# Perceiver layer on one core: queries of the scores dealt by ScalarE, the last 65 keys on all partition quarters, loads held back at the start

## The chip, the cores and the metric

One NeuronCore of a Trainium2 chip runs the whole layer. The metric is the device time of one execution in microseconds, as the median of several runs. All data is fp32.

## The reference, cut to what matters

A batch of 8 samples has 64 query rows each and 1,601 context rows (keys) of width 512. The layer is cross attention to the context with one head, a second attention over the 64 rows with 16 heads, and a feed-forward layer that sends every row to one of eight experts.

```python
# x: (8, 64, 512), ctx: (8, 1601, 512)
q = layernorm(x) @ Wq + bq
k = ctx @ Wk + bk;  v = ctx @ Wv + bv
x = x + softmax(q @ k.T / sqrt(512)) @ v
xn = layernorm(layernorm(x)) * ln_w + ln_b       # second attention, 16 heads of 32
qh, kh = l2norm(xn @ Wq2), l2norm(xn @ Wk2)
m = sigmoid(15 * (qh @ kh.T - 0.29514)) * (qh @ gq)[:, None] * (kh @ gk)[None, :]
x = x + (m @ (layernorm(x) @ Wv2)) @ Wo + bo
h = layernorm(x)                                 # experts
e, w = argmax(h @ gate.T), sigmoid(max(h @ gate.T))
x = x + expert_e(w * h)                          # u * silu(g) @ down
```

## The kernel before, in words

The 512 query rows are four tiles of 128 (p = 0 to 3); a tile holds two samples (b2 = 0, 1). The kernel never forms the keys: it computes q Wk^T once for a tile (`keyed`, p_qk, four products against the slab xWkT) and multiplies it with the raw context. The scores of a tile are summed over 16 blocks of 32 context columns, four blocks to a quarter q (`scores`, L369). The context arrives with keys on partitions, in three groups of 512 keys (a load of 1 MB for each sample, twelve keys of a sample on one partition, four of them per group) and a tail of 65 keys (`load_group`, L205 to L217). VectorE turns 32x32 blocks of it (`turn_group`, L231) into the tiles T: partition quarter a of T holds 32 columns by the keys whose row lies in partition quarter a, 384 of them plus the tail's share. The tail lies in partitions 0 to 64 of an array of 96 rows, so the four quarters have 416, 416, 385 and 384 keys (WIDTH, L226). TensorE then runs eight products at once, four row quarters by two samples, into four banks sc.

For that, the queries must stand four times under one another: R has 128 partitions (four quarters of the same 32 columns) by 16 blocks by 128 rows. GpSimd writes each 32 columns of q Wk^T four times side by side (`spread`, L341), TensorE turns 16 such squares (`fill_queries`, L358, rt) and ScalarE copies them to R in four copies (L361). R exists once.

`softmax` (L376) takes the four maxima on VectorE, a bias, and four exponentials on ScalarE into L, with a fifth of one column for key 65. `chances` turns L back (pp, L413), ScalarE copies it (pt, L415), and `attend` multiplies it with the context as it came (ac, L425), group by group. `divided` scales (acs), and the value projection xWv follows one tile later (`at_turn`, `at_out`, p_po).

Arrays live in pools: twelve slabs of 1 MB for weights and context groups, five block arrays (tag blk) for T, L and the blank rows, 22 rows of 256 KB. A load waits until its array is free. TensorE's order is the order in which the program is written; ScalarE's is so only from `keyed(0)` to the transposes of x; the other engines are ordered by a scheduler when the kernel is built. All large loads go through SP's queue, in order, and a load there waits until the eighth before it has landed. Small constants go through GpSimd's queue.

At the start the kernel normalizes x, projects tile 0's queries, forms q Wk^T of tile 0, then projects the other three tiles (`project_q`). VectorE meanwhile turns the first five T arrays of tile 0 as the loads arrive in the order tail, 0, 1, 2; xWv and tile 1's loads follow at once. After the scores of tile 0 come the q Wk^T of tiles 1, 2 and 3. From tile 1 on, the steps of the second attention and of the gate of earlier tiles are set between those of the cross attention: the gate's part (`gate_parts`, shares, L700; `gate`, pl) starts in tile 2.

## Time and profile before

| | us |
|---|---|
| median of 3 runs | 295.79 |
| lowest and highest | 295.11, 296.79 |
| profiled execution, its own time | 295.09 |
| its span | 293.4 |
| TensorE busy | 279.1 |
| VectorE busy | 159.6 |
| ScalarE busy | 93.2 |
| GpSimd busy | 63.9 |

The profile is of one execution. Durations and start times are counted from the start of its span; the execution's own time is 1.69 us longer than the span. A line of the timeline has the start, the duration, the engine (PE is TensorE, PEld its weight load, DVE VectorE, ACT ScalarE, POOL GpSimd, SP the engine of the load queue), the line of the kernel, and what is written from what. A group line has the busy time and the mean of one instruction after the first bar, and the idle time of the engine before them, with what ended it, after the second. A matmul of fp32 appears as two records.

### The profile page before, as it was taken

To read this page: it belongs to the slowest core of one execution; us is meant where nothing else is said; L and a number is where in the kernel's file an instruction comes from. 1 tells how busy PE (TensorE), PEld (TensorE's weight loads), DVE (VectorE), ACT (ScalarE), POOL (GpSimd) and SP (SyncE) were. 2 spreads that over 40 slices of the span, in tenths; PEclk is the share of its full clock that TensorE was granted. 3 is DMA by queue.
4 is the path that set the end of the run, shared out by engine and by line. 5 is a ranking of instruction groups with operands and counts; after the bars stand their busy time and mean duration, and the time that the engine had idled before them with its cause. 6 is when DMAs were issued, how large, how long until landed. Compare 5 with 4: busy or idle time off the path is not lost. (4 is left out here: it accounts for less than half of the span.)

```text
span 293.4 us, 6477 instructions
## 1 busy us (share of the span) xinstructions
PE 279.1 (95%) x2661; PEld 138.3 (47%) x2661; DVE 159.6 (54%) x414; ACT 93.2 (32%) x203; POOL 63.9 (22%) x110
## 2 busy tenths in 40 slices
PE   5689999999999999999999999999999999999991
PEld 5555664633554244655534465534454455343320
DVE  2554487336853477956667794453372466374140
ACT  3221403620037131326714143652425434130110
POOL 4055400600081002500220310022050032413301
PEclk9999999999999999999999999999999999999999
DMA  6999980189974993000199401959991200523401
GB/s 185 348 414 396 344 330 1 32 347 416 386 275 163 359 417 122 4 3 0 29 395 369 142 2 26 370 188 329 376 376 61 74 0 2 158 92 117 175 3 43
DMA packets 20288, 57.71 MB, mean 197 GB/s; under 512 B 2274, under 2 KB 10514, under 8 KB 16544
## 3 DMA queue, kind: packets, MB, share of 16 engines
q1 hardware_dynamic: 17568, 50.37, 47.5%
q0 software_dynamic: 2400, 6.89, 6.3%
q8 instruction: 23, 0.38, 0.5%
q14 instruction: 9, 0.07, 0.1%
q10 hardware_dynamic: 288, 0.00, 0.1%
HBM read 50.94 MB, written 6.84 MB: 197 GB/s over the span
## 5 line engine op out<-in xcount | busy, mean ns | idle before, releaser
L233 DVE STREAM_TRANSPOSE T<-cx 128x512 f32<-128x512 f32 x96 | 61.9, 681 | 25.1 <-DMA cx<-in_ctx_dram 19.4
L369 PE MATMUL sc<-T,R 32*64 32x416 f32 (+2 forms) x1024 | 49.9, 501 | 0.1
L425 PE MATMUL ac<-cx,pt 128*64 128x512 f32 x192 | 43.8, 599 | 0.0
L369 PEld LDWEIGHTS sc<-T,R 32*64 32x64 f32 x1024 | 26.5, 131 | 17.6 <-issue 6.8
L425 PEld LDWEIGHTS ac<-cx,pt 128*64 128x64 f32 x192 | 12.7, 136 | 22.1 <-issue 21.2
L1010 PE MATMUL gu<-wgu,xeT 128*32 128x512 f32 x192 | 22.9, 597 | 0.0
L501 POOL TENSOR_TENSOR gm_k<-qn_k,c_gk 128x512 f32<-128x512 f32 x4 | 5.1, 1284 | 61.4 <-DVE qn_k L496 61.4
L185 PE MATMUL p_qk<-w_xWkT,qpT 128*128 128x512 f32 x32 | 14.2, 598 | 2.9 <-DMA w_xWkT<-in_xWkT_dram 2.9
L464 POOL TENSOR_TENSOR x<-x,c_bo 128x512 f32<-128x512 f32 x4 | 5.1, 1268 | 53.6 <-DVE xh L463 53.6
L341 POOL COPY q<-qk 128x512 f32<-128x512 f32 x16 | 9.0, 615 | 34.0 <-ACT qk L313 34.0
L284 PE MATMUL qp<-xnT,w_xWq 128*128 128x128 f32 (+1 forms) x64 | 14.4, 384 | 1.3 <-ACT xnT L275 1.3
L185 PE MATMUL p_q<-w_aWq,xhT 128*128 128x512 f32 x32 | 14.8, 605 | 0.1
L185 PE MATMUL p_k<-w_aWk,xhT 128*128 128x512 f32 x32 | 14.7, 595 | 0.0
L185 PE MATMUL p_po<-w_xWv,acT 128*128 128x512 f32 x32 | 14.7, 595 | 0.0
L380 DVE TENSOR_REDUCE mx<-sc 128x1 f32<-128x416 f32 (+2 forms) x16 | 8.1, 567 | 11.9 <-PE sc L369 11.9
L185 PE MATMUL p_o<-w_aWo,cT 128*128 128x512 f32 x32 | 14.5, 596 | 0.0
L185 PE MATMUL p_v<-w_aWv,xvT 128*128 128x512 f32 x32 | 14.4, 592 | 0.0
L415 ACT COPY pt<-pp 128x512 f32<-128x512 f32 (+1 forms) x16 | 8.2, 515 | 17.5 <-PE pp L413 15.8
L284 PEld LDWEIGHTS qp<-xnT,w_xWq 128*128 128x128 f32 x64 | 9.7, 191 | 5.7 <-ACT xnT L275 1.8
L1045 PE MATMUL y<-wd,hT 128*32 128x512 f32 x96 | 11.5, 596 | 0.6 <-DVE hT L1037 0.6
L185 PEld LDWEIGHTS p_qk<-w_xWkT,qpT 128*128 128x128 f32 x32 | 5.8, 190 | 10.5 <-issue 7.4
L1020 DVE TENSOR_TENSOR h<-gu,h 128x256 f32<-128x256 f32 x6 | 2.5, 424 | 14.0 <-ACT h L1019 14.0
(198 smaller groups left out, 387.6 us busy)
## 6 DMA issues: line engine op xcount, KB each, us to landing
cx<-in_ctx_dram SPq DMA_DIRECT2D x24, 1024.0 KB, 10.1
wgu<-in_wgT_dram SPq DMA_DIRECT2D x8, 512.0 KB, 9.2
wgu<-in_wuT_dram SPq DMA_DIRECT2D x8, 512.0 KB, 10.0
wd<-in_wdT_dram SPq DMA_DIRECT2D x8, 512.0 KB, 8.4
rd<-blank POOLq DMA_DIRECT2D x6, 258.0 KB, 4.8
in<-rd SPq DMA_DIRECT2D x6, 258.0 KB, 5.0
xd<-blank POOLq DMA_DIRECT2D x6, 256.0 KB, 4.8
in<-xd SPq DMA_DIRECT2D x6, 256.0 KB, 7.2
```

The lines of the kernel that those rows point to most:

```text
L185: nc.tensor.matmul(ps, lhsT=srcT[:, dc, :], rhs=w[:, dc, :], start=(dc == 0), stop=(dc == DC - 1),)
L233: nc.vector.transpose(T[:, :, 128 * g : 128 * g + 128].rearrange("p b (c k) -> p b c k", k=32), cxs[p, g][b2][:, :, 128 * q : 128 * q + 12 ...
L284: nc.tensor.matmul(ps[ec][:, : n * P], lhsT=wq[:, dc, ec * P : (ec + 1) * P], rhs=xnT[:, dc, cols], start=(dc == 0), stop=(dc == DC - 1),)
L341: nc.gpsimd.tensor_copy(q4, qk[:, 32 * b0 : 32 * b0 + 128].rearrange("p (b d) -> p b d", d=32).unsqueeze(2).to_broadcast([P, 4, 4, 32]),)
L369: nc.tensor.matmul(sc[a][r : r + S, : WIDTH[a]], lhsT=R[32 * a : 32 * a + 32, b, r : r + S], rhs=Ts[b2][32 * a : 32 * a + 32, j, : WIDTH[a ...
L380: nc.vector.tensor_reduce(mx[:, a : a + 1], sc[a][:, : WIDTH[a]], AX.X, ALU.max)
L415: nc.scalar.copy(pt[:m, :nch, :], tp[:m, :nch, :])
L425: nc.tensor.matmul(ac[r : r + S, :], lhsT=pt[:m, j, r : r + S], rhs=rhs, start=(g == 0 and j == 0), stop=(g == 3),)
L464: nc.gpsimd.tensor_tensor(xs[i], xs[i], bo, ALU.add)
L501: nc.gpsimd.tensor_tensor(heads(gm), heads(qn), gb.unsqueeze(1).to_broadcast([P, H, HD]), ALU.mult)
L1010: nc.tensor.matmul(ps[c, :], lhsT=xTs[k][:, dc, c], rhs=ffw[e][0][:, dc, :], start=(dc == 0), stop=(dc == DC - 1),)
L1045: nc.tensor.matmul(y[c, :], lhsT=hT[:, ic, c], rhs=ffw[e][1][:, ic, :], start=(ic == 0), stop=(ic == IC - 1),)
```

## The change

Seven edits belong together:

- q Wk^T of tiles 1 to 3 is turned plainly, four transposes for a tile (`turn_queries`), and ScalarE deals it to R: for each partition quarter a, four copies of 32 partitions by 512 (`deal_queries`). Tile 0 keeps the old way.
- q Wk^T of tile 3 is formed in tile 1 instead of tile 0, and ScalarE's order is written by hand from the softmax's end to the end of the attend stage in tiles 0 to 2.
- In tile 0, VectorE's order is written by hand: groups 0, 3 and 1 of tile 1 are turned into four T arrays after the softmax, group 2 around `divided`.
- At the start, the transposes of x for tiles 1 to 3 stand between the two halves of tile 0's q Wk^T.
- The tail is loaded in pieces of 17, 16, 16 and 16 keys to the four partition quarters, so the score widths are 401, 400, 400, 400; the softmax treats it as a 13th column of 128 with zeros, and four small exponentials fill it.
- The tail's loads come behind groups 0 and 1 (four large loads) in tile 0.
- Two slabs are held by a one-column copy on GpSimd that reads the end of qpT, in front of the constants' loads; xWv is loaded after tile 1's context.

```diff
-        [one.tile([96, D], F32, tag=f"tail{k}{b2}", name=f"tail{k}{b2}") for b2 in range(2)]
+        [one.tile([P, D], F32, tag=f"tail{k}{b2}", name=f"tail{k}{b2}") for b2 in range(2)]
-            nc.gpsimd.memset(tails[k][b2][64:96, :], 0.0)
+            nc.gpsimd.memset(tails[k][b2], 0.0)
+    REST = (17, 16, 16, 16)
-                nc.sync.dma_start(out=c[: SK - 12 * P, :], in_=src[12 * P :, :])
+                k0 = 12 * P
+                for a, n in enumerate(REST):
+                    nc.sync.dma_start(out=c[32 * a : 32 * a + n, :], in_=src[k0 : k0 + n, :])
+                    k0 += n
-    for g in (3, 0, 1, 2):
+    for g in (0, 1, 3, 2):
         cxs[0, g] = load_group(0, g)
-    wv = load_w("xWv")
-    WIDTH = (416, 416, 385, 384)
+    WIDTH = tuple(384 + n for n in REST)
...
+    def turn_queries(p):
+        return transposed(qks.pop(p), f"rt_{p}")
+    def deal_queries(R, tp, a):
+        for j in range(4):
+            nc.scalar.copy(R[32 * a : 32 * a + 32, j::4, :], tp[32 * j : 32 * j + 32, :, :])
...
+        nc.gpsimd.memset(L[:, 12, :], 0.0)
...
-        nc.scalar.activation(
-            L[:, 12, 64:65], sc[2][:, 384:385], AF.Exp, bias=bias, scale=scale,
-            accum_out=sm[:, 4:5],
-        )
+        for a, n in enumerate(REST):
+            nc.scalar.activation(
+                L[:, 12, 32 * a : 32 * a + n], sc[a][:, 384 : 384 + n],
+                AF.Exp, bias=bias, scale=scale,
+            )
+        nc.vector.tensor_reduce(sm[:, 4:5], L[:, 12, :], AX.X, ALU.add)
...
-        keyed(0)
-        for i in range(1, NT):
-            turn_x(i, later[i - 1])
+        def turn_later():
+            for i in range(1, NT):
+                turn_x(i, later[i - 1])
+        keyed(0, turn_later)
...
+    for k in range(2):
+        tc.keep_in_program_order(
+            nc.gpsimd.tensor_copy(slab(f"held{k}")[:, 0, 0:1], qpT[:, DC - 1, NT * P - 1 :])
+        )
...
     load_pair(1)
+    wv = load_w("xWv")
...
+        if p > 0:
+            do((at_turn, p - 1))
         L, r = softmax(p, sc)
+        if p == 0:
+            turns = tc.manual_schedule(engines={mybir.EngineType.DVE})
+            turns.__enter__()
+            second = {(q, b2): block_tile(1, q, b2) for q in range(2) for b2 in range(2)}
+            for g in (0, 3, 1):
+                turn_second(g)
+        acts = ExitStack()
+        if p < NT - 1:
+            acts.enter_context(tc.manual_schedule(engines={mybir.EngineType.Activation}))
...
         if p == 0:
             for k in range(1, NT):
-                keyed(k)
-                if k == 1:
-                    q4s = spread(1)
+                if k < NT - 1:
+                    keyed(k)
+            turned_qk = turn_queries(1)
+            R = queries(1)
             tables()
...
-        if p + 1 < NT:
+        if p == 0:
+            chance()
+        elif p + 1 < NT:
             R = queries(p + 1)
-            if p == 0:
-                chance()
-                fill_queries(1, R, q4s, 0)
...
+            if p == 1:
+                keyed(NT - 1)
+            do((at_out, p - 1))
+            chance()
+            turned_qk = turn_queries(p + 1)
...
             attend(p, g, pts[g], ac)
+            if p < NT - 1 and g < 3:
+                deal_queries(R, turned_qk, g)
+                if p == 0 and g == 2:
+                    deal_queries(R, turned_qk, 3)
...
+        if p == 0:
+            turn_second(2, (0,))
         tile_of[p]["acs"] = divided(p, ac, r)
+        if p == 0:
+            turn_second(2, (1,))
         if 0 < p < NT - 1:
             do((unit_q, p - 1))
+            deal_queries(R, turned_qk, 3)
+        acts.close()
```

## The prediction

> **What bounds the kernel now.** I read the page's busy table first, then the groups by form, then the timeline around the places that the diff touches.

> ```profile
> PE 279.1 (95%) x2661; PEld 138.3 (47%) x2661; DVE 159.6 (54%) x414; ACT 93.2 (32%) x203; POOL 63.9 (22%) x110
> L369 PE MATMUL sc<-T,R 32*64 32x416 f32 x512 | 49.9, 513 | 0.1
> L358 PE MATMUL rt<-ident,q 128*128 128x128 f32 x64 | 8.0, 272 | 0.0
> L361 ACT COPY R<-rt 128x512 f32<-128x512 f32 x16 | 8.5, 601 | 1.2 <-PE rt L358 1.2
> ```

> PE is busy in 95% of the span, and its groups show almost no idle time before them: TensorE's order of work is the path, and the other engines count only where TensorE would come to wait for them. So I price each edit in TensorE time, and then look for what TensorE meets next. The stage in question is tile 0, from its last score matmul to tile 1's scores (start, duration, engine):

> ```profile
> 45.84 10.57 PE L185 MATMUL p_qk<-w_xWkT,qpT 128*128 128x512 f32 x24
> 45.94 2.02 DVE L380 TENSOR_REDUCE mx<-sc 128x1 f32<-128x416 f32 x4 [3.10 <-PE sc L369]
> ...
> 48.43 0.21 DVE L386 TENSOR_SCALAR bias<-qb,nb 128x1 f32<-128x1 f32 x1
> ...
> 48.72 1.28 ACT L391 ACT_TABLE_LOAD   x1 [15.66 <-DVE bias L386]
> ...
> 52.55 1.09 ACT L313 COPY qk<-p_qk 128x512 f32<-128x512 f32 x2
> ...
> 56.39 0.64 PE L413 MATMUL pp<-ident,L 128*128 128x128 f32 x4
> ...
> 56.86 1.91 PE L358 MATMUL rt<-ident,q 128*128 128x128 f32 x16
> ...
> 59.14 3.65 PE L425 MATMUL ac<-cx,pt 128*64 128x512 f32 x16
> ...
> 71.59 3.80 PE L369 MATMUL sc<-T,R 32*64 32x416 f32 x84
> 71.74 0.75 DVE L432 TENSOR_SCALAR acs<-ac,r 128x512 f32<-128x512 f32 x1 [1.21 <-PE ac L425]
> ```

> The reader is to see that three products p_qk (10.5 us) cover the softmax: its exponentials end at 52.3, pp follows at 56.39 without a wait. At the start the loads set the pace instead. The windows view gives GB/s in its last column:

> ```profile
> 12.00:15.00 3.00, 1.44 (x4) 0.68 (x4) 2.49 (x8) 0.52 (x2) 0.00 (x0) 1.00 1.05 296
> 16.00:20.00 4.00, 3.17 (x17) 2.04 (x16) 2.33 (x8) 2.05 (x4) 2.07 (x4) 1.00 1.02 424
> 32.50:36.50 4.00, 3.95 (x75) 1.87 (x64) 1.31 (x2) 0.30 (x2) 0.17 (x1) 1.00 1.02 284
> ```

> In the first and third of these a pair of 65-row tail loads is in flight, and everything crawls: 296 and 284 GB/s against 424. VectorE's timeline has tile 0's groups arriving 2.5 us apart (turned at 18.55, 21.02, 23.52), then 3.3, 2.8 and 3.2 us apart while GpSimd's constants load; the last is turned at 32.85, and the scores, started at 32.66, stop for it.

> [...] the table load's 1.28 us stands in the trace. [...] a quarter of the scores (64 records) takes 2.95 us start to start here.

> **The change part by part.** Every change of time is against the profiled execution, 295.09 us (span 293.4 and 1.7 around it); the median of the runs, 295.79, lies 0.7 above it.

> 1. *Queries by ScalarE.* Tiles 1 to 3 lose 16 transposes each and gain 4. The 16 take 1.75 us (56.86 to 58.61), four take 0.45: **1.3 us less of TensorE each, 3.9 in all.** ScalarE gets 16 copies of 0.51 us (8.2 us) in place of 4. Their cover is the attend stage, 12.4 us with 1.6 us of other copies in tile 0: three quarters are dealt beside groups 0 to 2, the fourth beside group 2 (tile 0) or the next products (tiles 1, 2). The last copy of tile 0 ends about when its first scores need it: nothing to pay (2.1 us, the last quarter's four copies, if that cover is gone). But in tile 2, four deals (2.1 us) now stand ahead of the square-root table load and the copy of the gate's shares, which today ends 0.04 us before TensorE uses it (145.32, 145.36): **0.7 us of wait.** In tile 1 the same copies have slack, since no gate is computed there. GpSimd's 12 copies of 0.6 us go; they ran beside p_qk and the scores, so nothing.

> 2. *One product p_qk moved from tile 0 to tile 1.* TensorE's sum is the same, but the cover in tile 0 shrinks from 10.5 to 6.95 us. In the changed order four turns of tile 1 (two of 0.66, two of 0.27 us) also stand between the maxima and the bias on VectorE, 1.5 us of them unhidden. From the last score S: bias at S+4.3 (now S+2.8), table load 1.3, four exponentials 2.25, four small ones 0.8 ([...] a lone one takes 0.24 here with its accumulator), copy of the product and hand-over 0.75: S+9.4. TensorE is there at S+6.95: **a new wait of 2.4 us at the transposes of q Wk^T.** Then 0.45 for them, 0.15, pp 0.45 and its copy: attend starts at S+11.2, now at S+13.3, **2.1 us earlier**. Tile 1 pays: between its scores and pp stand 0.5 + 3.47 + 3.47 = 7.45 us instead of 5.3 (which held a 0.45 us wait for the exponentials): **2.15 us later**.

> 3. *Turns of tile 1 ahead.* Group 2 of tile 1 is loaded once tile 0's first attend group frees its buffers, lands 4.9 and 7.4 us later (as the load issued at 56.44 did: turned at 61.37), so the first quarter is ready as the scores start: 0.2 us. Then VectorE has acs (0.75), two turns (1.25) and four blocks of 2.05 us, 10.2 us, before the last quarter can run (2.85): 13.2 us for tile 1's scores instead of 12.2: **1.0 us later.** VectorE becomes the bound there.

> 4. *Narrower scores.* 401 columns for 416: 2.95 becomes 2.85 us a quarter. Eight quarters in tiles 2 and 3: **0.8 us less.** Tiles 0 and 1 wait for VectorE's blocks in their last quarter and keep nothing.

> 5. *Tails, holds and start.* Without the tails in front, groups land earlier by 0.65 us of bytes and 0.85 of lost rate (0 to 1.9 as bounds); the constants move behind qpT, which takes 0.85 us off group 1. So the fourth large load lands at about 24.3. Now a wait is added on SP's queue: the last of eight tail pieces waits for that landing, and group 2's loads stand behind it[...]. Issue at 24.8 to 26, landing 4.9 us later, the second 2.5 after: 32.2 to 33.4, now 32.85. [...] TensorE itself is ready some 1.4 us sooner (the first half of xWkT lands 0.6 earlier; with the transposes between the halves the 0.8 us wait for xnT goes). I take **0.7 us less**, between 1.4 less and 2.5 more. The tails cost SP six more issues a tile of some 0.35 us; its queue has waits of tens of us, so nothing but the stop above. The two held copies on GpSimd wait for qpT (30.6), and behind them the seven constant loads and four additions of xbv move from 20 to 33 us on to about 31 to 43; their first user is tile 0's output sum near 89. Tile 1's loads, xWv and the attention weights come later than now, under tens of us of other work. The output weight and tile 2's first group wait for the moved product; the normalization of tile 1's stage stands behind that group on VectorE, with 1 to 3 us to spare by my count.

> 6. *Softmax details.* A memset of 0.2 us on GpSimd, idle then, and one more reduce beside pp and attend: nothing. Tail transposes and products have as many columns as before: nothing.

> Sum: 1.3 (tile 3's queries) − 0.7 in tile 2; 2.1 − 0.2 in tile 0; −1.0 − 2.15 + 0.45 (queries and their copies after pp) in tile 1; 0.8 for scores; 0.7 at the start: **1.3 us less**. 295.09 − 1.3 = 293.8 in the profile, **294.5** as median. Of 5.4 us taken off TensorE's work, three new waits take most back.

> **The rivals.** *The cover holds.* If maxima, turns and exponentials overlap better, and the blocks of tile 1 arrive in time, 2.4 + 1.0 and half of the 0.7 us of waits vanish: 3.75 us more, 290.8. For it: the exponentials end 4 us before pp today. Against: the product's copy stands behind the exponentials on ScalarE. *The start gets slower.* Group 2 issued behind the tail pieces: [...] the last group lands at 35.4, 2.5 us late. The rest of the sum gives 0.6, so 1.9 us slower: 297.7. It decides from a landing at 35.0. For it: issue waits in order on SP; against: the crawl at 296 GB/s ends. *The edits don't pay in TensorE time*: the array's rate isn't set by the width, and tile 2's first group comes late: 295.8.

> **How the numbers follow.** Forecast 0.46 (own range 292.9 to 296.1), cover holds 0.22, slower start 0.22, no gain 0.10. The bound for a difference that a measurement of this kernel can tell is about 0.5%, 1.5 us: 294.3 and 297.3. Half of the forecast's chance lies below 294.3, the rest within; with the rivals: faster 0.46, same 0.30, slower 0.24. Leaving out one in ten on each side gives 290.6 to 297.8.

> **What would show it.** Right: a wait of some 2 us of the transposes t_rt for ScalarE's copy of qk in tile 0; the scores of tile 1 over 13 us, waiting for VectorE's T; 12 fewer query transposes in each of tiles 1 to 3; no stretch under 300 GB/s at 12 to 15 us, but a dip near 25 to 27. Wrong: the first scores starting after 34, or pp of tile 0 within 9 us of the last score.

## The result and the profile after

| | before | changed |
|---|---|---|
| median, us | 295.27 (20 runs) | 296.41 (20 runs) |
| lowest to highest, us | 294.04 to 297.12 | 294.39 to 298.27 |
| profiled execution, its span, us | 295.09, 293.4 | 296.17, 294.4 |

The changed kernel takes 1.0035 times as long, with an interval of 1.0014 to 1.0055: about 1.0 us slower, where 1.3 us less was forecast. Ratios here are of undisturbed executions alone, so a ratio can differ from that of two medians.

The busy table and the groups of the changed kernel show that the edits did what they say:

```profile
PE 277.9 (94%) x2625; PEld 134.9 (46%) x2625; DVE 160.5 (55%) x418; ACT 116.0 (39%) x247; POOL 58.1 (20%) x104
...
L382 PE MATMUL sc<-T,R 32*64 32x400 f32 (+1 forms) x1024 | 50.7, 516 | 3.2 <-DVE T L237 2.2
...
L374 ACT COPY R<-t_rt 32x512 f32<-32x512 f32 x48 | 27.6, 576 | 0.8
```

TensorE has 36 records fewer (12 transposes for each of three tiles), and ScalarE has 48 deals. But the score group now has idle time ahead of it, 3.2 us in all, 2.2 of them on VectorE's T. TensorE's timeline shows where (start, duration, engine, line, what is written from what, count; in brackets the idle time just before, and what ended it). First the kernel before, then the changed one:

```profile
32.66 3.97 PE L369 MATMUL sc<-T,R 32*64 32x416 f32 x64
36.57 0.33 PE L332 MATMUL t_qb<-ident,qbT 128*128 128x128 f32 x1
```
```profile
29.78 1.08 PE L324 MATMUL qb<-qpT,c_xbk 128*32 128x128 f32 x32
31.05 0.85 PE L382 MATMUL sc<-T,R 32*64 32x401 f32 x2 [0.19 <-DVE T L237]
33.96 4.63 PE L382 MATMUL sc<-T,R 32*64 32x401 f32 x62 [2.05 <-DVE T L237]
38.52 0.33 PE L336 MATMUL t_qb<-ident,qbT 128*128 128x128 f32 x1
...
47.70 7.13 PE L185 MATMUL p_qk<-w_xWkT,qpT 128*128 128x512 f32 x16
```

TensorE comes to tile 0's first scores 1.6 us sooner than before (31.05 for 32.66), runs two records, waits 2.05 us, and then takes 4.63 us for the other 62; later quarters take 2.94 for 64. The windows view of the same stretch gives the reason in its third column from the right, the granted clock (then DMA share and GB/s):

```profile
30.69:34.10 3.41, 1.16 (x18) 0.33 (x18) 2.31 (x5) 0.27 (x1) 2.27 (x5) 1.00 0.92 280
34.10:37.52 3.42, 3.42 (x48) 1.72 (x52) 0.40 (x1) 0.00 (x0) 2.29 (x2) 0.50 0.73 217
```

From 34.10 to 37.52 us TensorE has half its clock. In the run with the short filler below, the same 62 records take 2.94 us at full clock, so this costs 1.69 us, half of the 3.42 us within rounding. Without it the first quarter would have ended 0.26 us later than before (38.52 less 1.69 for 36.57). VectorE's and SP's timelines show why TensorE waited. VectorE before, for the last load, then VectorE and SP in the changed kernel:

```profile
32.85 1.31 DVE L233 STREAM_TRANSPOSE T<-cx 128x512 f32<-128x512 f32 x2 [1.29 <-DMA cx<-in_ctx_dram]
```
```profile
20.50 1.90 DVE L237 STREAM_TRANSPOSE T<-cx 128x512 f32<-128x512 f32 x3 [1.19 <-DMA cx<-in_ctx_dram]
24.77 1.30 DVE L237 STREAM_TRANSPOSE T<-cx 128x512 f32<-128x512 f32 x2 [2.37 <-DMA cx<-in_ctx_dram]
...
30.19 1.90 DVE L237 STREAM_TRANSPOSE T<-cx 128x512 f32<-128x512 f32 x3 [2.81 <-DMA cx<-in_ctx_dram]
33.19 1.30 DVE L237 STREAM_TRANSPOSE T<-cx 128x512 f32<-128x512 f32 x2 [1.10 <-DMA cx<-in_ctx_dram]
```
```profile
6.03 3.44 SPq L214 DMA_DIRECT2D cx<-in_ctx_dram  x4
9.87 15.21 SPq L219 DMA_DIRECT2D tail<-in_ctx_dram  x8
25.12 0.90 SPq L214 DMA_DIRECT2D cx<-in_ctx_dram  x2
```

The eight tail pieces stand 15.2 us in SP's queue, and group 2 is issued only at 25.12. The last four pieces start their issue at 15.57, 18.00, 20.49 and 24.77 us, just after the last landing records of the four large loads, each eight loads ahead in the queue (15.50, 17.98, 20.48 and 24.75). Meanwhile the DMA engines have little to do, 82 GB/s:

```profile
21.50:26.00 4.50, 4.50 (x15) 2.66 (x14) 2.13 (x4) 0.00 (x0) 0.00 (x0) 1.00 0.34 82
```

Group 2's last load lands at 33.17 and is turned from 33.19 on, 0.34 us later than before.

After the start the changed kernel is the faster one. S is again the start of the products p_qk, the end of tile 0's scores:

| us, from the profiles | before | changed | difference |
|---|---|---|---|
| S | 45.84 | 47.70 | +1.86 |
| S to tile 0's attend | 13.30 | 10.82 | −2.48 |
| tile 1's scores | 12.24 | 13.03 | +0.79 |
| tile 1, last score to pp | 5.24 | 7.29 | +2.05 |
| tile 1, pp to tile 2's scores | 25.79 | 25.37 | −0.42 |
| tile 2's scores to tile 3's | 50.56 | 49.94 | −0.62 |
| tile 3's scores to the last product y | 120.08 | 119.98 | −0.10 |

With tile 0's attend itself (+0.01) all below the first row comes to −0.77, and with the start to +1.09. The waits of TensorE, as the waits view lists them (total, times, longest):

```profile
PE sc L382 <- DVE T L237: 2.2, 2, 2.1
...
PE t_rt L177 <- ACT qk L317: 1.7, 1, 1.7
PE sc L382 <- DVE T L244: 1.0, 1, 1.0
...
PE pl L719 <- ACT shares L711: 0.5, 1, 0.5
```

The three lower ones were forecast. So the question is the start.

The kernel's own executions point the same way. Of its 20, the five with a mean granted clock of 0.995 or more average 294.9 us, the other fifteen 296.9. That mean is a rough mark: it also falls where TensorE stands idle at the end (the profiled execution with the short filler keeps its clock until TensorE's work runs out, and has 0.994).

### The profile page after: what moved, and what is told of

It reads as the page before. It is cut to its first block, busy times and chain, and to the rows that moved or that the text cites. A ratio compares the mean times of both kernels' runs of the same rounds, so it can differ in the third digit from the quotient of the medians.

```text
span 294.4 us, 6471 instructions
## 1 busy us (share of the span) xinstructions
PE 277.9 (94%) x2625; PEld 134.9 (46%) x2625; DVE 160.5 (55%) x418; ACT 116.0 (39%) x247; POOL 58.1 (20%) x104
## 5 line engine op out<-in xcount | busy, mean ns | idle before, releaser
L382 PE MATMUL sc<-T,R 32*64 32x400 f32 (+1 forms) x1024 | 50.7, 516 | 3.2 <-DVE T L237 2.2
L382 PEld LDWEIGHTS sc<-T,R 32*64 32x64 f32 x1024 | 25.7, 135 | 22.7 <-issue 15.3
L374 ACT COPY R<-t_rt 32x512 f32<-32x512 f32 x48 | 27.6, 576 | 0.8
L288 PE MATMUL qp<-xnT,w_xWq 128*128 128x128 f32 (+1 forms) x64 | 15.7, 412 | 0.5 <-ACT xnT L279 0.5
L185 PE MATMUL p_q<-w_aWq,xhT 128*128 128x512 f32 x32 | 14.8, 606 | 0.2 <-DVE xhT L483 0.2
L185 PE MATMUL p_k<-w_aWk,xhT 128*128 128x512 f32 x32 | 14.7, 596 | 0.0
L185 PE MATMUL p_qk<-w_xWkT,qpT 128*128 128x512 f32 x32 | 14.6, 598 | 0.0
L185 PE MATMUL p_po<-w_xWv,acT 128*128 128x512 f32 x32 | 14.6, 592 | 0.0
L185 PE MATMUL p_o<-w_aWo,cT 128*128 128x512 f32 x32 | 14.5, 596 | 0.0
L185 PE MATMUL p_v<-w_aWv,xvT 128*128 128x512 f32 x32 | 14.4, 592 | 0.0
L288 PEld LDWEIGHTS qp<-xnT,w_xWq 128*128 128x128 f32 x64 | 11.1, 221 | 5.3 <-ACT xnT L279 0.9
L393 DVE TENSOR_REDUCE mx<-sc 128x1 f32<-128x400 f32 (+1 forms) x16 | 8.1, 565 | 8.2 <-PE sc L382 8.2
```

The lines of the kernel that those rows point to most:

```text
L185: nc.tensor.matmul(ps, lhsT=srcT[:, dc, :], rhs=w[:, dc, :], start=(dc == 0), stop=(dc == DC - 1),)
L288: nc.tensor.matmul(ps[ec][:, : n * P], lhsT=wq[:, dc, ec * P : (ec + 1) * P], rhs=xnT[:, dc, cols], start=(dc == 0), stop=(dc == DC - 1),)
L374: nc.scalar.copy(R[32 * a : 32 * a + 32, j::4, :], tp[32 * j : 32 * j + 32, :, :])
L382: nc.tensor.matmul(sc[a][r : r + S, : WIDTH[a]], lhsT=R[32 * a : 32 * a + 32, b, r : r + S], rhs=Ts[b2][32 * a : 32 * a + 32, j, : WIDTH[a ...
L393: nc.vector.tensor_reduce(mx[:, a : a + 1], sc[a][:, : WIDTH[a]], AX.X, ALU.max)
```

## The experiments

The theory: TensorE's dry spell at the first scores costs it the clock, and this is the loss. The rivals: the late data themselves; the new waits further on; an accident of single executions.

**A long filler on TensorE.**

```
             if p == 0 and q == 0:
+                idle_turns(24)
```

> 24 transposes of the identity (some 2.6 us of TensorE) are put ahead of tile 0's first scores, so that TensorE has work while it waits for the last turned groups; the data arrive as before. Theory A, the clock: TensorE runs dry for 2.05 us before the first scores, and that is why it is granted half the clock for 3.4 us. With the filler the granted clock stays at 1.0 from 34 to 37.5 us, the first quarter of tile 0 takes 2.9 us instead of 4.6, and the kernel ends 1.6 us earlier: 294.8. Rival B, the data: the scores' first quarter is slow because its blocks are late, filler or not; it ends at 38.5 as in the changed kernel: 296.4. Rival D, an accident: the clock falls in as many executions as in the changed kernel, whatever TensorE did before.

Measured: 295.36 us (22 runs), ratio to the kernel before 0.9984 (0.9959 to 1.0009), where the changed kernel had 1.0035: about 1.5 us less.

```profile
32.21 2.84 PE L118 MATMUL idle<-ident 128*128 128x128 f32 x24
34.98 2.94 PE L382 MATMUL sc<-T,R 32*64 32x401 f32 x64
```

The clock stays full and the first quarter takes 2.94 us. In this execution TensorE came to its scores 1.2 us later than in the changed kernel's profile, since its clock rose later at the very start (its first products qp take 6.32 us for 5.21), so its S is 47.70 again; the gain is in the ratio. A mean granted clock of 0.995 or more was seen in 15 of 22 executions, in the changed kernel in 5 of 20, in the kernel before, run beside it, in 42 of 75. Against an accident of one execution also stands that the three other profiles with the changed kernel's start (the third product back, tile 3's queries by TensorE, full width, all below) lose the clock there too, at 33.69, 32.51 and 35.62 us.

**A short filler.** The same line with `idle_turns(8)`.

> The changed kernel with 8 transposes of the identity (0.95 us) ahead of tile 0's first scores instead of 24: the data come no earlier and TensorE still waits, but only 1.1 to 1.2 us. If the clock is set by how much of a window of 3.41 us TensorE was idle (windows with up to 1.75 us idle were followed by full clock, those with 2.02 us or more by half), it stays at 1.0 from 34 to 37.5 us and the first quarter takes 2.9 us: as good as the long filler, 1.5 us less than the changed kernel, 294.9. Rival: any wait just there costs the clock, or the wait itself is the loss: 296.4, with the half clock in the record.

Measured: 294.53 us (20 runs), ratio 0.9992 (0.9965 to 1.002), 1.3 us less than the changed kernel by the ratios. The two intervals overlap a little; those of the long filler and of the changed kernel don't.

```profile
33.61 2.94 PE L382 MATMUL sc<-T,R 32*64 32x401 f32 x62 [1.93 <-DVE T L237]
```

In this profile the wait is still 1.93 us, so the expectation of 1.2 was wrong: the full clock began at 5.5 us here and at 10.2 in the changed kernel's profile, so TensorE came to its scores sooner. But the wait falls into two of the windows of 3.41 us by which the clock records go (1.12 and 0.82 us, reckoned with the records' ends; last section), the clock stays full, and S is 45.66. Nearly the same wait with and without the clock's fall: the fall is what costs. It is not gone from all executions: ten of 20 have a mean clock of 0.995 or more and average 294.0 us, the other ten 295.9.

**Group 2 ahead of the tails.**

```
-    for g in (0, 1, 3, 2):
+    for g in (0, 1, 2, 3):
         cxs[0, g] = load_group(0, g)
...
-        for g in (0, 1, 3, 2):
+        for g in (0, 1, 2, 3):
             for b2 in range(2):
```

> The loads of tile 0's group 2 go ahead of the eight tail pieces (order 0, 1, 2, tails), and the turns on VectorE in the same order; the held constants, widths and all else stay. Theory A: the stop of SP's queue behind the tail pieces is gone, large loads follow each other 2.5 us apart, the last is turned at about 28 and TensorE, ready at 31.05, does not wait and keeps its clock. Tile 0's last score comes 3 to 4.5 us earlier than in the changed kernel, where VectorE's blocks do not take some of it back; the end 2.9 (T) and up to 1.6 (clock) earlier, I say 3.5 less: 292.9. Rival E, the pieces of 17 rows: they now land last, [...] behind the large loads, and TensorE waits for the turned tails until 33 or later: within 0.5 of the changed kernel, 296.

Measured: 295.30 us (22 runs), ratio 0.9953 (0.9924 to 0.9981), 2.4 us less than the changed kernel by the ratios, not 3.5.

```profile
30.10 1.30 DVE L237 STREAM_TRANSPOSE T<-cx 128x512 f32<-128x512 f32 x2 [1.51 <-DMA cx<-in_ctx_dram]
```

The stop is gone: from 21.5 to 26 us 421 GB/s are moved, for 82, and group 2's last load is turned from 30.10 on, 3.1 us sooner. Rival E holds in part: the tails come last, TensorE waits 0.92 and 1.22 us for their turns (L244), together over 2 us in one window, and in the profiled execution the clock falls at 33.7. Ten of 22 executions had a mean clock of 0.995 or more.

**Tails on ScalarE's queue**, to free SP's.

```
-    for g in (0, 1, 3, 2):
+    for g in (0, 1, 2):
         cxs[0, g] = load_group(0, g)
...
         turn_x(0, normal([0])[0])
+        cxs[0, 3] = load_group(0, 3, nc.scalar)
```

> Tile 0's eight tail pieces are issued from ScalarE's queue, in its idle time after the first four copies of xnT (about 8 us), so that on SP's queue group 2's loads follow group 1's at once; the turns keep the order 0, 1, tails, 2. If the start is the whole loss (theory A): group 2 is issued at about 10.5 us instead of 25.1, its second load lands at 28.7 to 30.2 and is turned by 30.9, when TensorE is ready; no wait over 0.3 us, no half clock; the first quarter takes 2.9 us and tile 0's last score ends near 43.4 instead of 47.7; the kernel ends 4.3 us earlier than the changed one: 292. Rival F: the pieces, in front now, delay xWkT and TensorE's own start by 0.7, and tile 0's scores then run into VectorE's blocks: last score at 45.5, 294.2. Rival B, the start is not the loss: within 0.5 of the changed kernel.

Measured: 314.04 us (6 runs), ratio 1.0636 (1.0587 to 1.0684). All three expectations missed. ScalarE's timeline:

```profile
12.11 20.53 ACTq L219 DMA_DIRECT2D tail<-in_ctx_dram  x8
32.74 1.14 ACT L293 ACTIVATE qpT<-qp,c_xbq 128x128 f32<-128x128 f32 x4 [25.32 <-DMA tail<-in_ctx_dram]
```

The stop moved with the pieces. ScalarE's issues stretch over 20.5 us, as SP's had over 15.2, and the qpT of tile 0 stands behind them. TensorE's first p_qk waits 20.25 us for it.

**Tails issued by GpSimd**, which is idle from 4 to 18 us. The group is loaded with `nc.gpsimd`, ahead of the large ones in the program.

> Tile 0's eight tail pieces are issued by GpSimd at 3 to 8 us, where it has nothing else to do, so that neither SP's large loads nor ScalarE's copies stand behind them. Theory A, the start is the whole loss: group 2 is issued right behind group 1, its last load is turned by 30.9, TensorE (ready between 30.9 and 31.5) waits less than 0.5 us, the clock stays full, tile 0's last score comes at about 43.5 instead of 47.7, and the kernel ends 4 us earlier than the changed one and 2 to 3 earlier than the one before: 292.3, ratio 0.991. Rival F: the pieces, 0.65 us of bytes [...], come in front of xWkT; TensorE starts p_qk 1 us later and VectorE's blocks bound tile 0's scores: last score at 45.5, 294.3. Rival B, the start is not the loss: 296.4.

Measured: 295.82 us (14 runs), ratio 1.0008 (0.9981 to 1.0035). S is 44.76, 2.94 us sooner than in the changed kernel, with no wait at the first scores and a full clock:

```profile
32.69 2.94 PE L383 MATMUL sc<-T,R 32*64 32x401 f32 x64
```

That is between the 43.5 expected and the 45.5 of rival F, which holds in part: with the pieces in front, the first half of xWkT lands at 14.56 us (11.77 in the changed kernel), the first p_qk starts at 14.70 for 12.35, and TensorE comes to the scores at 32.69, 1.6 us later. That the wait is gone is owed to both, data 1.6 us sooner (last turn from 31.59 on) and a later TensorE. From S to the last product y, moreover, this kernel takes 240.56 us (changed kernel 238.89). A wait of the second attention's query product in tile 1 takes 1.9 of it, where the changed kernel has 0.2:

```profile
104.89 3.27 PE L185 MATMUL p_q<-w_aWq,xhT 128*128 128x512 f32 x7 [1.90 <-DVE xhT L484]
```

VectorE's order puts two of the four parts of xhT behind turns of tile 2's first loads. The second of these loads is turned from 100.89 on, only 1.27 us sooner than in the changed kernel (102.16), and eight turns run before the first part. Step 5 of the prediction had given this place 1 to 3 us to spare. A start nearly 3 us sooner uses that up.

**Constants not held back.** The two held copies on GpSimd are left out.

> The changed kernel without the two copies that hold GpSimd's constant loads back until qpT is complete, so that these loads run from about 4 us on, between the large ones. If holding them is worth what the prediction put down (0.85 us on group 1), group 1's loads land 0.5 to 0.9 us later than 20.5 and 24.8; group 2's issue, which waits for group 1's last landing, moves by as much, and TensorE waits 2.5 to 3 us at the first scores. Rival: the constants fit into the stretch from 21 to 26 us in which the DMA engines are nearly idle, and nothing moves.

One execution, 303.90 us. The constants start at 20.7, not at 4 (they stand behind GpSimd's copies of q). Group 1 moves by half a microsecond one way and the other (21.00 and 24.36), but the second sample's tail is turned at 28.93 for 26.87 and group 2 at 31.99 and 35.06 for 30.19 and 33.19; S is 50.52. The holds are worth 1.9 us at the last group, and here the clock's fall at 34.4 lasts two windows. A wait of 3.0 us for xhT follows, and a second fall at 112.9.

**The third product q Wk^T back in tile 0.** Its call is back in tile 0's loop, and that in tile 1 is gone.

> The third product of q with Wk^T goes back from tile 1 to tile 0's stage, where it was in the kernel before. Theory A: the 1.7 us wait at tile 0's query transposes goes, tile 0 takes 13.2 us from its last score to attend instead of 10.8, and tile 1 takes 5.0 from its last score to pp instead of 7.4: +2.4 - 2.4, no change, 296.4 within 0.5. The wait was nothing that the move had cost in sum. Rival C, the new waits eat the gain: the 1.7 us of waiting come back and the kernel ends 1.7 earlier, 294.7.

Measured: 296.18 us (22 runs), ratio 0.9997 (0.9969 to 1.0025). In the profile S to attend takes 12.30 us (+1.48) and tile 1's last score to pp 5.44 (−1.85); from S to tile 2's scores it is 0.62 less than in the changed kernel. Neither expectation: moving the product to tile 1 costs some 0.6 us in this profile, because the wait of 1.75 us at t_rt eats half of the 3.44 us of products that leave tile 0. The interval of the ratio is too wide to confirm 0.6.

**Tile 3's queries by TensorE again.**

> Tile 3's queries are turned by TensorE again (GpSimd spreads q Wk^T, 16 transposes, 4 copies by ScalarE), tiles 1 and 2 stay with ScalarE's deals. Theory: TensorE has 12 transposes more in tile 2's stage, 1.3 us, and the 0.5 us wait of the gate's product for ScalarE's copy of the shares goes: tile 2 from its last score to the end of its attend takes 0.8 us more (24.7 for 23.9). Rival: the copies and transposes hid under other waits in tile 2, and the stage takes as long as it did.

One execution, 296.92 us. From tile 2's last score to the end of its attend 24.47 us for 23.91: +0.56, near the 0.8 expected. But tile 3's scores then take 15.12 for 15.45, since the products al (the second attention's scores) no longer wait for kT there. The queries of tile 3 by ScalarE gain the 0.6 forecast in tile 2's stage and give 0.3 of it back in tile 3's scores, 0.2 net.

**Full width for the scores.** All score products over 416 columns.

> The score products read 416 columns in each row group, as the widest did before the change, in place of 401 and 400; all else stays. If the widest of the four row groups sets the pace, a quarter of tile 2's and tile 3's scores takes 0.08 us more (2.95 for 2.87), 0.64 in eight quarters, and some 0.1 in tiles 0 and 1, which wait for VectorE: 297.1. Rival: the rate is not set by the width but by the issue of the 64 products: no change, 296.4.

Measured: 297.35 us (22 runs), ratio 1.0021 (0.9994 to 1.0049), which tells neither apart. The records do, here and in the changed kernel, for the first quarter of tile 3, both at full clock:

```profile
168.92 3.05 PE L382 MATMUL sc<-T,R 32*64 32x416 f32 x64
```
```profile
166.61 2.94 PE L382 MATMUL sc<-T,R 32*64 32x401 f32 x64
```

The width sets the pace: 0.11 us a quarter. With 416 columns in two of the four row groups, as before, such a quarter takes 3.02.

**The wait at t_rt taken away.** First beside the tails on ScalarE, then beside those on GpSimd: tile 1's q Wk^T is copied by VectorE, and the bias comes ahead of the turns. What `between` calls is keyed(1), with VectorE's copy, and then the four turns.

```
     def softmax(p, sc, between=None):
...
+        if between is not None:
+            between()
         nc.vector.tensor_reduce(sm[:, 4:5], L[:, 12, :], AX.X, ALU.add)
```

> As the kernel with tile 0's tail pieces on ScalarE's queue, and in tile 0's stage the copy of tile 1's q Wk^T goes from ScalarE (behind the exponentials) to VectorE, the bias ahead of the four turns. Theory: the 1.75 us wait of the query transposes comes from the copy's place behind the exponentials and from the turns ahead of the bias. Bias at S+2.9 (S is the start of the products p_qk; now S+4.0), exponentials done at S+7.2 (now 8.2), transposes at S+7.1 without a wait over 0.3, attend from S+9.2 (now 10.8): 1.6 us earlier than the kernel with the tails on ScalarE alone. Rival: VectorE, which bounds tile 1's scores (a wait of 1.0 us for its blocks), gets 0.6 us more to do and the earlier start is waited out there: tile 1's scores take 14.5 us instead of 13.0 and nothing is gained.

> As the kernel with the tails issued by GpSimd, with the copy of tile 1's q Wk^T on VectorE and the bias ahead of the four turns. Beside the tails on ScalarE these took the attend of tile 0 from S+10.5 to S+8.9 us after the last score, but 1.1 us of it came back as a wait of the attention's query product for VectorE's xhT in tile 1. Theory: tile 2's first group, on which VectorE's order stands, follows a load whose time is fixed by the loads ahead; the 1.1 us come back here too, 0.6 us less than the kernel with GpSimd's tails alone: 291.7. Rival: the wait was due to that kernel's start 20 us late, and the full 1.6 us stay: 290.7.

With ScalarE's tails: 311.98 us (6 runs), ratio 1.0579, and S to attend 8.87 us where the tails alone had 10.51: the 1.6 us expected. With GpSimd's tails: **293.65 us** (22 runs), ratio 0.9932 (0.991 to 0.9953). S to attend is 8.86; p_q waits 1.6 us for xhT, less than beside the tails alone, so the rival, that the full 1.6 us stay, is the better one here (S to last y 238.35 for 240.56). Both of its absolute times, 291.7 and 290.7, took a start for granted that the tails alone had not brought.

**xhT by ScalarE for tile 0.**

```
-            if dc % 2 == 0:
+            if i > 0 and dc % 2 == 0:
                 nc.vector.tensor_scalar(
```

> As the kernel with the tails issued by GpSimd and the copy of q Wk^T on VectorE; for tile 0 alone, all four parts of the normalized, turned sums (xhT) are made by ScalarE instead of two of them by VectorE, where they stand behind seven turns of tile 2's groups. If that place on VectorE is what holds the attention's query product now, its wait of 1.6 us goes (ScalarE is idle from 98.5 us, and the transposes t_xh end at 99.9), from the end of tile 1's attend to tile 2's scores it takes 10.6 us as before the start was repaired (now 12.1), and the kernel ends 1.5 us earlier: 292.2. Rival: VectorE is behind in tile 2's blocks, so the 1.5 us come back as waits of tile 2's scores for T or of al for kT: 293.6.

Measured: **292.31 us** (11 runs), ratio 0.9892 (0.986 to 0.9924), faster than both kernels.

```profile
101.29 1.08 PE L438 MATMUL ac<-tail,pt 128*64 128x512 f32 x4
102.30 3.70 PE L185 MATMUL p_q<-w_aWq,xhT 128*128 128x512 f32 x8
```

p_q follows without a wait, and the end of attend to tile 2's scores takes 10.43 us (10.6 expected). That shows the second path: VectorE's order ties xhT to tile 2's loads. The start is not at its best here either: in this profile, with the tail pieces still in front, the first p_qk waits 3.41 us for xWkT, and the clock falls at 15.05 us, so that S is 46.11.

## Why the prediction was wrong

**The step that failed is 5, the start**: 0.7 us less was put down, and 1.86 more was measured. It failed in two places.

- *The transfer.* The prediction reckoned the last landing at 32.2 to 33.4, and it came at 33.17; the load is turned 0.34 after the 32.85 of before. The stop on SP was seen, with its place and length. But 0.7 less does not follow from such a landing: TensorE's being ready sooner gains nothing while the last group sets the start.
- *The clock.* That TensorE, ready 1.6 us sooner, would stand still for 2.05 us was the price not seen. The wait itself moved the start little, but it cost the clock, 1.69 of the 1.86 us. The prediction put down no fall of the clock. Both fillers show what the fall costs: in their profiles the last load is turned 0.70 us later (long) and 0.35 sooner (short) than in the changed kernel's, the clock stays, and the ratio goes from 1.0035 to 0.9984 and 0.9992.

The other steps held in mechanism. The signs that the prediction named for itself came: the wait at t_rt, tile 1's scores waiting for VectorE, the 12 transposes fewer, 421 GB/s at 12 to 15 us for 296, and a dip, 96 GB/s from 25 to 27. What the crawl of before came from, no run shows. In brackets what was forecast:

- **Step 1.** The shares cost a wait of 0.55 (0.7), pp to tile 2's scores gained 0.42 (0.45), and tile 2 gained 0.61 from its last score to the end of attend (0.6). A deal of 32 partitions takes 0.576 us, where a copy of 128 to R took 0.601 before, and four deals take 2.34 us (2.1, an estimate).
- **Step 2.** The wait at t_rt took 1.75 us (2.4), attend came at S+10.8 (11.2), and tile 1's last score to pp took 2.05 more (2.15). The four small exponentials of tile 0 take 0.63 us, from 55.27 to 55.90 (0.8, an estimate).
- **Step 3.** Tile 1's scores took 13.0 us (13.2), with a wait of 1.0 for VectorE's T and none of the first quarter (0.2).
- **Step 4.** A quarter takes 2.87 us from start to start (2.85), for 2.95 before, which is 0.64 in eight. That the width sets the pace was an estimate; the run at full width shows it (3.05 us at 416 columns, 2.94 at 401). But with the products al now waiting for kT, the score stages of tiles 2 and 3 take 15.60 and 15.45 us, for 15.61 and 15.39 before, and nothing is left of it. In tile 3 that wait is gone in the one run in which TensorE turns the queries.
- **Step 6.** No cost is seen.

The sum after the start was forecast at −0.6 and measured at −0.77. In part that is luck: tiles 0 and 1 came out some 0.9 us better than forecast, tiles 2 and 3 some 0.7 worse.

In step 5 the hold of the constants was undersized: 1.9 us at the last group in the one run without it, where 0.85 was put down, at group 1. Without the hold the start would have been slower still.

Of the rivals, "the start gets slower" named the right place, group 2 behind the tail pieces, but priced it by a landing at 35.4, an estimate, 2.2 us later than measured. Of the 2.5 us that it put down at the start 1.86 came, but nearly all of it by the clock, which it didn't name. "The cover holds" is refuted: all three waits came. "The edits don't pay in TensorE time" is refuted in its reason, since the width does set the rate, and right in that nothing of the narrower scores is left; tile 2's first group comes late by 0.2 us of waiting here, by 1.9 with the tails on GpSimd.

What is shown: the clock's fall after the wait, what it costs, and that group 2 is late because of the stop on SP. Open is why a start 2.9 us sooner brings VectorE's second load of tile 2 only 1.27 us forward.

## What to carry to other kernels

Making an engine ready sooner gains nothing where a transfer sets the pace, and on TensorE it can lose: a stall of 2 us has cost 1.7 more in clock here, so either close it or fill it. Ask of every load that is moved which issues on its queue wait for earlier landings, and what else of that engine stands behind them; eight small pieces held SP for 15 us and ScalarE for 20. And after a start is repaired, look for the next place where an engine's order is tied to a load.
